# Last instruction of quantising the FFN weights: from VectorE to ScalarE

## The chip, the cores and the metric

The kernel runs on one core of a Trainium2 chip. The metric is the device time of one execution in microseconds. Six names are used for the parts of the core. PE is TensorE (matrix multiplies), and PEld is its loading of weights. DVE is VectorE, ACT is ScalarE, POOL is GpSimd, and SP is SyncE, whose queue (SPq) issues every DMA of this kernel. Each engine carries out its own instructions in order, and waits at an instruction until what that instruction needs has been done by the others.

## The reference

One layer with gated cross-attention and a gated feed-forward part (FFN), for 32 sequences of 224 tokens of width 512, with a context of 750 rows of width 384 for each sequence:

```
x = x + tanh(g_xattn) * attention(layernorm(x), ctx, mask, Wq, Wkv)     # 16 heads of 32
x = x + tanh(g_ffn)   * ffn(layernorm(x), w1, b1, w2, b2)

def weight_quant(w):
    scale = 1.0 / clip(mean(abs(w)), 1e-05)
    return clip(round(w * scale), -1.0, 1.0) / scale
def bitlinear(x, w, b):
    return act_quant(rmsnorm(x)) @ weight_quant(w).T + b
ffn = bitlinear(gelu(bitlinear(x, w1, b1)), w2, b2)
```

The two FFN weights (2048 x 512 and 512 x 2048) are replaced by one of -1, 0, 1 times the mean of their absolute values. The mean is a sum over the whole matrix, so a weight has to be read once for its mean and again to be rounded.

## The kernel before, in words

The work is a loop over 128 steps (32 sequences times 4 groups of 4 heads), written out at build time from line 908 on. Each step takes about 20 us and has six slots, k = 0 to 5. The order of the instructions on every engine is the order of the calls in the code: the wrapper `Ordered` (lines 44 to 52) records every call in program order, which is why nearly all rows of the profile carry the line number 52.

In the even slots, `maxima` (line 308) of the *next* step writes scores to PSUM on PE (tile `sm`), and DVE takes their maximum (tile `mx`, one reduction of about 2.24 us). In the odd slots, `weights` (line 365) of the *current* step writes the scores again on PE (tile `se`), and ACT takes the exponential (tile `p`, 1.66 us), which POOL adds up (tile `acc`, passes of about 2.1 us). `sm` and `se` share one PSUM buffer (pool `ps_s`, line 164). So PE, DVE and ACT pass it round: `sm` waits until ACT has read `se`, and `se` waits until DVE has read `sm`.

In the slots lie further pieces. `k_units` (line 260) computes keys two steps ahead; ACT copies them to `kT`, in slots 0 and 1. `v_piece` (line 276) computes values, which ACT or DVE copies. `q_piece` (line 249) computes queries, multiplied into `qT` by DVE. `turn_max` in slot 0 gives `nT`, copied by ACT, which the `se` of slot 1 needs. `finish` on POOL gives `yo`, and `store` on SP writes it to memory in slot 4. In the first step of a sequence, slot 4 also has `spread` (line 235): SP writes 224 numbers to memory (`r_d`), and reads them back to all partitions (`rb`). These pieces use the four PSUM buffers of pool `ps_m` in turn.

The FFN weights are prepared in the first twelve steps by `weight_units` (line 447). It gives 34 units, and one of them is called in each odd slot, after `weights` of that slot and before its other pieces. First come sixteen units that load a piece of 128 x 1024 numbers (`fetch`, SP) and add up its absolute values (`add_up`, DVE). Then one unit works out the scales. Then sixteen units load each piece again and quantise it (`quantise`, line 486). These last units are numbered 0 to 15 in what follows. They fall on steps 6 to 11: units 0, 3, 6, 9, 12, 15 have slot 1, units 1, 4, 7, 10, 13 slot 3, and units 2, 5, 8, 11, 14 slot 5. (Unit 0 comes in slot 1 of step 6, since the unit ahead of it, with the scales and the first load, has slot 5 of step 5.)

Each unit first issues the load of the piece of the next unit. The pieces lie in the two buffers of tag `h` (line 455). So the load for unit n + 1 waits until unit n - 1 has finished with its piece. `quantise` has three instructions: times the scale and at most 1; at least -1 and plus `MAGIC` (12582912, which rounds to a whole number); and minus `MAGIC`, with the result written in 8 bits to `w1q` or `w2q`. The tile `magic` (line 107) holds -`MAGIC` in each partition. The FFN proper (`Ffn.fill`) starts after these units, and the first matrix multiply that reads `w1q` is at 368 us.

Of the kernel before, what the change touches and what calls it, by code (L numbers as in the profile page):

```python
# [13 lines left out]
AF = mybir.ActivationFunctionType  # L14
ALU = mybir.AluOpType
# [5 lines left out]
MAGIC = 12582912.0  # L21
# [3 lines left out]
def flamingo_gated_layer(  # L25
# [28 lines left out]
    pe, dve, act = Ordered(nc.tensor), Ordered(nc.vector), Ordered(nc.scalar)  # L54
# [52 lines left out]
    magic = const.tile([P, 1], F32, name="magic")  # L107
# [339 lines left out]
    def weight_units():  # L447

        NW = 8
        parts = const.tile([P, 2, NW], F32, name="wparts")  # L450
        tot = const.tile([P, 2], F32, name="wtot")
        held = {}

        def fetch(which, i, tag):
            wl = hp.tile([P, F // 2], F32, tag="h", name=f"{tag}_{which}_{i}")
            if which == 0:
                c, h = divmod(i, NW // NDC)
                n = F * NDC // NW
                sp.dma_start(wl, w1T[c * P : (c + 1) * P, h * n : (h + 1) * n])
                held[tag, which, i] = wl, w1q[:, c, h * n : (h + 1) * n]  # L460
                return
            k = NFC // NW
            sp.dma_start(
                wl.rearrange("p (k d) -> p k d", k=k),
                w2T[i * k * P : (i + 1) * k * P, :].rearrange("(k p) d -> p k d", p=P),
            )
            held[tag, which, i] = wl, w2q[:, i * k : (i + 1) * k, :].rearrange("p k d -> p (k d)")

        def add_up(which, i):
            wl, _ = held.pop(("wa", which, i))  # L470
            dve.tensor_reduce(
                parts[:, which, i : i + 1], wl, AX.X, ALU.add, apply_absolute_value=True
            )

        def mean():
            dve.tensor_reduce(tot, parts, AX.X, ALU.add)
            pm = ps_m.tile([P, 512], F32, tag="m", name="pwm")
            pe.matmul(pm[:, 0:2], ones, tot, start=True, stop=True)
            dve.tensor_scalar(wmean, pm[:, 0:2], 1.0 / (D * F), 1e-5, ALU.mult, ALU.max)
            dve.reciprocal(wscale, wmean)  # L480

            dve.tensor_scalar(w127, wmean, 1.0 / 127.0, None, ALU.mult)
            dve.tensor_tensor(w127[:, 1:2], w127[:, 1:2], tg[:, 1:2], ALU.mult)
            dve.tensor_scalar(b2g, b2g, tg[:, 1:2], None, ALU.mult)

        def quantise(which, i):
            wl, to = held.pop(("wb", which, i))
            dve.tensor_scalar(wl, wl, wscale[:, which : which + 1], 1.0, ALU.mult, ALU.min)
            dve.tensor_scalar(wl, wl, -1.0, MAGIC, ALU.max, ALU.add)
            dve.tensor_scalar(to, wl, -MAGIC, None, ALU.add, saturate=False)  # L490

        every = [(w, i) for w in range(2) for i in range(NW)]
        units = [lambda: fetch(*every[0], "wa")]
        for n, wi in enumerate(every):
            def one(n=n, wi=wi):
                if n + 1 < len(every):
                    fetch(*every[n + 1], "wa")
                add_up(*wi)
            units.append(one)

        def between():
            fetch(*every[0], "wb")
            mean()
        units.append(between)
        for n, wi in enumerate(every):
            def two(n=n, wi=wi):
                if n + 1 < len(every):
                    fetch(*every[n + 1], "wb")
                quantise(*wi)
            units.append(two)  # L510
        return units
# [509 lines left out]
```

## Time and profile before

| | us |
|---|---|
| three runs: median | 3109.46 |
| lowest, highest | 3102.85, 3111.33 |
| the profiled execution: its own time | 3101.86 |
| its span in the trace | 3100.1 |
| PE busy | 2902.6 (94%) |
| POOL busy | 2072.0 (67%) |
| DVE busy | 1745.1 (56%) |
| ACT busy | 1392.6 (45%) |
| stretch 170 to 240: PE, DVE, ACT busy of 70 | 64.16, 51.74, 20.87 |
| stretch 240 to 310: PE, DVE, ACT busy of 70 | 58.87, 46.58, 20.29 |

The profile shows one execution. Its durations and moments are used for sums, and the medians of the runs for what the time is. Times within the trace are counted from the start of the span. The sixteen units of `quantise` lie between 181.7 and 303 us. Outside this stretch no instruction is touched by the change. A row of the timeline gives the start, the duration, the engine, and in square brackets how long the engine had been idle and which instruction ended that. In a row of waits stand the total in us, how often, and the longest.

### The profile page before, as it was taken

To read this page: it belongs to the slowest core of one execution; us is meant where nothing else is said; L and a number is where in the kernel's file an instruction comes from. 1 tells how busy PE (TensorE), PEld (TensorE's weight loads), DVE (VectorE), ACT (ScalarE), POOL (GpSimd) and SP (SyncE) were. 2 spreads that over 40 slices of the span, in tenths; PEclk is the share of its full clock that TensorE was granted. 3 is DMA by queue.
4 is the path that set the end of the run, shared out by engine and by line. 5 is a ranking of instruction groups with operands and counts; after the bars stand their busy time and mean duration, and the time that the engine had idled before them with its cause. 6 is when DMAs were issued, how large, how long until landed. Compare 5 with 4: busy or idle time off the path is not lost.

```text
span 3100.1 us, 62640 instructions
## 1 busy us (share of the span) xinstructions
PE 2902.6 (94%) x26774; PEld 1843.6 (59%) x26774; DVE 1745.1 (56%) x2641; ACT 1392.6 (45%) x1344; POOL 2072.0 (67%) x2675
## 2 busy tenths in 40 slices
PE   8988899999999999999999999899999999999965
PEld 5655556665666666666666666566666656666543
DVE  5566555554655555555555555555555555555545
ACT  2322345454544545454444454545444454544543
POOL 3545767667676776776766767766767777667671
PEclk9999999999999999999999999999999999999987
DMA  4333221232221222221222222122221222222122
GB/s 135 94 102 101 51 43 45 63 71 54 57 59 39 66 62 68 66 50 38 61 54 62 61 71 57 30 69 48 73 61 35 53 68 62 71 64 45 23 51 65
DMA packets 352696, 190.02 MB, mean 61 GB/s; under 512 B 282144, under 2 KB 305056, under 8 KB 352288
## 3 DMA queue, kind: packets, MB, share of 16 engines
q1 hardware_dynamic: 352416, 186.01, 23.7%
q8 instruction: 209, 3.42, 0.5%
q14 instruction: 71, 0.58, 0.1%
HBM read 119.86 MB, written 29.39 MB: 48 GB/s over the span
## 4 chain that ended last, share of the span: by engine, by line
PE 78%; ACT 7%; DVE 5%; POOL 4%; DMA 4%; issue 2%; SPq 1%; ACTq 0%; POOLq 0%; DVEq 0%
PE po L52 16%; PE se L52 13%; PE pk L52 12%; PE sm L52 12%; PE pv_None L52 10%; PE ph L52 6%; ACT p L52 5%; PE pq L52 4%; DVE mx L52 4%; PE pv L52 3%; POOL acc L52 2%; ACT L52 1%; DMA r_d<-ve 1%; POOL xg L52 1%; POOL h L52 1%
## 5 line engine op out<-in xcount | busy, mean ns | idle before, releaser
L52 POOL TENSOR_TENSOR acc<-acc,p 125x896 f32<-125x896 f32 x512 | 1067.1, 2084 | 532.8 <-ACT p L52 512.6
L52 DVE TENSOR_REDUCE mx<-sm 112x4 f32<-112x2000 f32 (+1 forms) x384 | 861.0, 2242 | 627.7 <-PE sm L52 627.0
L52 ACT ACTIVATE p<-se 125x1792 f32<-125x1792 f32 x384 | 639.2, 1664 | 680.8 <-PE se L52 651.4
L52 PE MATMUL pk<-y,wkv_sb 128*128 128x375 f32 x1536 | 543.9, 490 | 9.6 <-DMA y<-in_ctxT 9.6
L52 PE MATMUL sm<-kT,qT 32*112 32x500 f32 (+1 forms) x4096 | 426.9, 508 | 72.2 <-ACT p L52 65.7
L52 POOL TENSOR_TENSOR acc<-p 125x896 f32<-125x896 f32 x128 | 268.9, 2101 | 269.9 <-ACT p L52 269.9
L52 PEld LDWEIGHTS pk<-y,wkv_sb 128*128 128x128 f32 x1536 | 277.3, 191 | 179.3 <-issue 43.0
L52 PE MATMUL pv_None<-wkv_sb,y 128*125 128x256 f32 x1548 | 368.0, 387 | 0.0
L52 PE MATMUL se<-qT,kT 32*125 32x224 f32 x6144 | 361.6, 351 | 0.0
L52 PEld LDWEIGHTS pv_None<-wkv_sb,y 128*125 128x125 f32 x1548 | 280.2, 187 | 131.3 <-issue 92.0
L52 PE MATMUL po<-p,v 125*32 125x224 f32 x6144 | 318.5, 356 | 0.0
L52 PEld LDWEIGHTS se<-qT,kT 32*125 32x125 f32 x6144 | 297.4, 184 | 0.0
L52 PEld LDWEIGHTS sm<-kT,qT 32*112 32x112 f32 x4096 | 159.4, 170 | 231.4 <-ACT p L52 172.7
L52 ACT COPY kT<-pk 128x375 f32<-128x375 f32 x256 | 119.9, 468 | 350.8 <-PE pk L52 350.5
L52 PE MATMUL ph<-w1q,xT 128*128 128x512 fp8e4 x896 | 228.6, 387 | 35.6 <-DMA xT<-xq 35.0
L52 DVE SCALAR_TENSOR_TENSOR h<-ph,qa_am,b_sb 128x512 f32<-128x512 f32 x224 | 165.5, 746 | 165.5 <-PE ph L52 160.4
L52 PEld LDWEIGHTS po<-p,v 125*32 125x32 f32 x6144 | 187.0, 110 | 119.6 <-issue 43.8
L52 PE MATMUL po<-w2q,hT 128*128 128x256 fp8e4 x1792 | 222.4, 280 | 25.5 <-DMA hT<-hq 22.6
L52 PE MATMUL pq<-xTb,wq_sb 128*128 128x224 f32 x1024 | 220.8, 359 | 1.1 <-DVE wq_sb L52 0.6
L52 PEld LDWEIGHTS <-hT 128*128 128x128 bf16 x1792 | 172.3, 100 | 66.4 <-DMA hT<-hq 24.5
L52 PE MATMUL se<-nT,ones 3*125 3x448 bf16 x1536 | 158.1, 401 | 49.2 <-DVE mx L52 42.4
L52 PEld LDWEIGHTS pq<-xTb,wq_sb 128*128 128x128 f32 x1024 | 189.3, 191 | 23.3 <-issue 12.4
(118 smaller groups left out, 2811.4 us busy)
## 6 DMA issues: line engine op xcount, KB each, us to landing
y<-in_ctxT SPq DMA_DIRECT2D x31, 1125.0 KB, 6.8
x<-in_x SPq DMA_DIRECT2D x32, 448.0 KB, 7.6
xTb<-in_xT SPq DMA_DIRECT2D x32, 448.0 KB, 3.8
o_d<-yo SPq DMA_DIRECT2D x512, 28.0 KB, 1.6
xg<-in_x SPq DMA_DIRECT2D x28, 512.0 KB, 3.7
og<-o_d SPq DMA_DIRECT2D x28, 512.0 KB, 4.6
out<-xg SPq DMA_DIRECT2D x56, 256.0 KB, 2.2
wa<-in_w1T SPq DMA_DIRECT2D x8, 512.0 KB, 7.1
```

The costliest lines, as they stand in the source:

```text
L52: return lambda *args, **kw: tc.keep_in_program_order(build(*args, **kw))
```

## The change

The third instruction of `quantise` is issued on ACT, as an activation with the function Identity and `magic` as its bias. It computes what the VectorE instruction computed (the piece plus -`MAGIC`), and writes the same tile in the same 8-bit type. Nothing else is changed.

```
             dve.tensor_scalar(wl, wl, wscale[:, which : which + 1], 1.0, ALU.mult, ALU.min)
             dve.tensor_scalar(wl, wl, -1.0, MAGIC, ALU.max, ALU.add)
-            dve.tensor_scalar(to, wl, -MAGIC, None, ALU.add, saturate=False)
+            act.activation(to, wl, AF.Identity, bias=magic, saturate=False)
```

## The prediction

> **What bounds the kernel now.** I read the busy shares first, then PE's waits, then the timeline of the stretch with the sixteen units. The share, and the wait that matters here:
>
> ```profile
> PE 2902.6 (94%) x26774; PEld 1843.6 (59%) x26774; DVE 1745.1 (56%) x2641; ACT 1392.6 (45%) x1344; POOL 2072.0 (67%) x2675
> ```
>
> ```profile
> PE se L52 <- DVE mx L52: 42.4, 47, 7.8
> ```
>
> PE sets the time; what counts is where PE stands still. Its wait for DVE's `mx` has single cases of up to 7.8 us. Between 170 and 310 us three of them lie right behind `quantise`. The first, from the timeline of 190 to 200 us:
>
> ```profile
> 190.39 0.75 DVE L52 TENSOR_SCALAR wb<-wb,wscale 128x1024 f32<-128x1024 f32 x1 [1.82 <-DMA wb<-in_w1T]
> ...
> 190.58 4.98 POOL L52 TENSOR_TENSOR acc<-acc,p 125x896 f32<-125x896 f32 x2 [4.75 <-ACT p L52]
> 191.18 2.45 DVE L52 TENSOR_SCALAR wb<-wb 128x1024 f32<-128x1024 f32 x1
> ...
> 193.66 2.45 DVE L52 TENSOR_SCALAR w1q<-wb 128x1024 fp8e4<-128x1024 f32 x1
> ...
> 196.03 0.38 DVE L52 TENSOR_TENSOR qT<-pq,rb 128x224 f32<-128x224 f32 x1
> 196.34 2.23 DVE L52 TENSOR_REDUCE mx<-sm 112x4 f32<-112x2000 f32 x1
> ...
> 198.61 0.64 PE L52 MATMUL se<-nT,ones 3*125 3x448 bf16 x4 [4.23 <-DVE mx L52]
> ```
>
> The reader is to see two things. The second and third instruction of `quantise` take 2.45 us each while POOL's two passes run; elsewhere the same instructions take 0.69. And PE waits 4.23 us for a reduction whose input (`sm`, 190.49 plus 1.11) had been there since 191.6. The other two stalls, from DVE's and PE's timelines of the stretch after 236 us:
>
> ```profile
> 244.74 2.52 DVE L52 TENSOR_SCALAR w2q<-wb 128x1024 fp8e4<-128x1024 f32 x1
> 247.18 2.23 DVE L52 TENSOR_REDUCE mx<-sm 112x4 f32<-112x2000 f32 x1
> 259.97 0.75 DVE L52 TENSOR_SCALAR wb<-wb,wscale 128x1024 f32<-128x1024 f32 x1 [10.56 <-DMA wb<-in_w2T]
> 260.75 0.69 DVE L52 TENSOR_SCALAR wb<-wb 128x1024 f32<-128x1024 f32 x1
> 261.48 0.69 DVE L52 TENSOR_SCALAR w2q<-wb 128x1024 fp8e4<-128x1024 f32 x1
> 262.09 2.23 DVE L52 TENSOR_REDUCE mx<-sm 112x8 f32<-112x2000 f32 x1
> ```
>
> ```profile
> 249.46 0.41 PE L52 MATMUL se<-nT,ones 3*125 3x448 bf16 x4 [1.66 <-DVE mx L52]
> ...
> 264.38 0.64 PE L52 MATMUL se<-nT,ones 3*125 3x448 bf16 x4 [7.83 <-DVE mx L52]
> ```
>
> In the second (unit 8) a POOL pass again stretches the third instruction, to 2.52 us. In the third (unit 9) DVE waits for a load; the instruction to be moved is the last thing ahead of `mx`.
>
> **What is removed.** Sixteen DVE instructions: 8 x 0.913 + 8 x 0.922, or 14.7 us busy. Most of it is worth nothing: in thirteen of the units DVE waits for PE again ahead of its next `mx`, or the `se` behind comes no later than usual (0.2 us of waiting). Three places count.
>
> Unit 1. `qT` starts at 193.66 instead of 196.03, so `mx` and `se` come 2.37 us earlier; 1.86 us of the stall are left. After 4.23 us of idle time the granted clock was 0.50 (198 to 202 us), and from `se` to the next `sm` took 203.78 - 198.61 = 5.17 us; the same stretch one step later, at full clock, took 224.16 - 221.11 = 3.05. So 2.12 us more are won if the clock now holds, 4.49 in all. Does it? The Trainium skill ("TensorE: Matmul & The Clock Gate", rules) wants no idle gaps above some 3 us; by it 1.86 is safe. The trace is less kind: after an idle gap of 2.46 us at 34 us the clock was 0.57 (36 to 40 us), while after 1.66 us at 249 it was 1.00 (250 to 254 us). 1.86 is nearer to the latter, so I take 4.49; the lower end is 2.37. The upper end is 6.35 (4.23 + 2.12): the load of unit 1 lands among other transfers, and were it some 0.6 us earlier, DVE's second instruction would start ahead of POOL's pass. The load behind it goes out later now (below), which could do that.
>
> Unit 8. `mx` follows `sm` again (1.17 us from `sm`'s start in the undisturbed steps: 244.54 + 1.17 = 245.71), and `se` could start at about 248.0, 1.45 us earlier. But the next stall waits for a transfer that was issued at 252.93, behind the `r_d` write of 246.03; none of that depends on unit 8's third instruction. PE reaches that stall earlier and waits longer: 0.
>
> Unit 9. `mx` starts when the second instruction ends, at 261.4 instead of 262.09: 0.69. The load itself may come earlier. It stands behind `r_d`, `store` and POOL's `yo`. One small POOL instruction beside unit 7's third instruction took 0.65 us where its like take 0.20, so `yo` is 0.45 earlier without it (between 0 and 0.9, as `yo` itself took 1.02 where it usually takes 0.56, beside unit 8). I take 0.45.
>
> **What is added.** Sixteen ACT instructions of 128 x 1024 with a bias from a tile. The nearest row has the same function, bias tile and size, with 16 bits out:
>
> ```profile
> L52 ACT ACTIVATE xq<-xc,magic 128x1024 bf16<-128x1024 f32 x28 | 32.1, 1147 | 20.7 <-POOL xc L52 19.5 <-DMA o_d<-yo 1.2
> ```
>
> 16 x 1.147 = 18.4 us on an engine that is busy 41 of these 140 us. No trace row has ACT writing 8 bits; I take 1.147 (0.9 to 2.3 as bounds: the mean of the DVE row, and twice the row). The Trainium skill ("ScalarE: Activation LUTs", rules for kernel authors) says to add on VectorE and not on ScalarE. By that rule, with the plain durations, the move loses 16 x (1.147 - 0.694) = 7.2 us if both engines were on the path. Here the row decides otherwise: ACT idles, and POOL's passes stretch the DVE form to 2.45 us. Between the start and 370 us ACT loads a table once, for the tanh at the very start, though Identity (`xc`, 329.90 us) follows the exponential there: no table is loaded for the change.
>
> **The new wait and what is behind it.** The ACT instruction stands after `p` of its slot, and waits for DVE's second instruction. Usually that is done before `p` ends (unit 5: 223.41 against 224.11), so it runs as soon as ACT is free. Behind it:
>
> ```profile
> 222.44 1.67 ACT L52 ACTIVATE p<-se 125x1792 f32<-125x1792 f32 x1 [0.63 <-PE se L52]
> 225.50 0.35 ACT L52 COPY nT<-pn 128x224 bf16<-128x224 bf16 x1 [1.40 <-PE pn L52]
> ```
>
> - Slot 5: `nT`, which the next `se` needs. 224.11 + 1.147 = 225.26, so it is free 0.24 us before `nT` can start. `se` starts at 227.63 and `nT` ends at 225.85, so 1.8 us more are in hand.
> - Slot 1: the copy to `kT` comes 0.85 us later, in unit 9 some 10 us later (262.6 instead of 252.75). The keys are read in the next step, and the PSUM buffer is needed again four pieces later (the value piece from 273.8 us on). Nobody waits.
> - Slot 3: ACT has 4 us free ahead of its next copy. In unit 1 the copy of `v` (194.42) is 0.4 us late, for a buffer that is not next.
>
> Where DVE's second instruction is late, `mx` is behind it on DVE as well and needs 2.24 us, longer than the ACT instruction and `nT` together (1.5).
>
> SP's queue: the load for unit n + 1 now waits for ACT in unit n - 1. That is 0.5 to 0.8 us later (unit 2's load: 184.65 instead of 183.9), at most 2.1 (unit 5's: 211.4 instead of 209.3). Loads land in a median of 4.6 to 5.5 us and are wanted 10 us after that. Behind them in the queue is `store`, which waits for POOL and comes later still. The tightest is unit 13's load, issued at 277.21 behind those of the next sequence: ACT is done with unit 11 at 275.7 + 1.15 = 276.85, 0.36 us before. Cost 0.
>
> **The sum.** 4.49 + 0.69 + 0.45 = 5.63 us. Against the profiled execution: 3101.86 - 5.63 = 3096.2, a ratio of 0.9982. That execution was 7.6 us below the median of the runs, so scaled to the median: 3109.46 x 0.9982 = 3103.8.
>
> **Rivals.** Less than 0.3% (9.3 us) is about what a measurement of this kernel can't tell from no change.
>
> 1. More is won (0.15). The locks between DVE and POOL fall differently in each execution, and the median of the runs is 7.6 us above the profiled one: it may hold more such stalls, in slots 3, where DVE's instructions come just ahead of POOL's passes (unit 13: 289.81 against 289.34). With unit 1's stall gone wholly (6.35) and one more of its kind (4.49): 12 us, 3097.5. Against: the order is fixed, and the trace has one such case among five.
> 2. It is hidden or given back (0.22). The clock drops anyway at 1.86 us, and PE's head start is lost at the next transfer, as I say of unit 8 (the load at 350 us, before a stall of 7.68): between 0 and 2.4 us won, 3107 to 3109.5.
> 3. Slower: ACT writes 8 bits far slower than 16 (0.05). The place is slot 5, where `nT` stands behind it. `nT` must end by 227.55, so an instruction of up to 227.55 - 0.35 - 224.11 = 3.1 us does no harm. Beyond that each of five units delays `se` by the excess. At 4.2 us the gain is eaten; at 6 us it is 5 x 2.9 = 14.5 - 5.6 = 9 us slower, 3118. Against: the row of 1.147, and 2048 elements take ACT 1.997 us with 16 bits out (`hq`) and 1.912 with 32 (`h`), so the width of the output hardly shows.
> 4. Unit 13's load comes late (0.08). Were ACT done with unit 11 2 us later than I say, unit 13's two instructions would both meet POOL's passes, as unit 1's did with 4.1 us of stall and 2.1 of cold clock: 6.2 - 5.6, no gain, 3110.
>
> **How the numbers follow.** The likeliest case, 3103.8, has 0.50. Its own range is 3099 to 3109, from the ends of the unit 1 and unit 9 terms and about 3 us of scatter of a median. A fifth of it, half of rival 1 and little else fall below 3100.1, which is 0.3% faster: 0.1 + 0.09, so 0.20. Above 3118.8 lie most of rival 3 and a tail of rival 4 and of the scatter: 0.07. The rest, 0.73, is within 0.3%. The range for 8 in 10 goes from half of rival 1 to the whole of rivals 2 and 4: 3095 to 3112.
>
> **What would show it.** In the changed profile: 16 ACT rows `w1q<-wb` and `w2q<-wb` of about 1.15 us, none stretched; PE's first stall in this stretch about 1.9 us, with `se` after it at full clock; the stall near 249 about 0.2; the stall of unit 9 about 8 us, since it takes over what unit 8 gives. `nT` and `kT` wait for nothing new. Wrong would be: table loads before 300 us, ACT rows above 3 us, a `se` that waits for `nT`, a longer wait of unit 13 for its load, or a gain in this stretch that is gone by 400 us.

## The result, and the profile after

The changed kernel takes 3102.22 us (median of 22 runs, 3096.14 to 3107.68), the kernel before 3105.9 us (median of 22 runs beside them). The ratio is 0.999, with a 95% interval of 0.9982 to 0.9998. So by the ratio the change gains 3 us (0.6 to 5.6), and the medians lie 3.7 us apart. That is little, but it is a gain. The prediction had said 3103.8 us and a ratio of 0.9982, that is 5.63 us.

The profiled execution after has a span of 3102.6 us, 2.5 *longer* than the one before. Single executions scatter by some 4 us, so the change has to be looked for where it acts. PE's waits in the profile after (total in us, how often, longest):

```profile
PE sm L52 <- ACT p L52: 66.1, 76, 3.1
PE se L52 <- DVE mx L52: 38.9, 48, 7.4
...
PE se L52 <- ACT nT L52: 5.0, 1, 5.0
```

PE's wait for `mx` is 42.4 - 38.9 = 3.5 us shorter, and its wait for `nT` is what it was before (5.0 us, once, in both). The moved instruction costs ACT what the row with 16-bit output said (groups, mean in ns after the busy time):

```profile
L52 ACT ACTIVATE w2q<-wb,magic 128x1024 fp8e4<-128x1024 f32 x8 | 9.1, 1142 | 9.3 <-DVE wb L52 9.3
L52 ACT ACTIVATE w1q<-wb,magic 128x1024 fp8e4<-128x1024 f32 x8 | 9.1, 1141 | 6.4 <-DVE wb L52 6.4
```

Unit 1 in the timeline after, DVE's rows and then PE's:

```profile
192.58 0.75 DVE L52 TENSOR_SCALAR wb<-wb,wscale 128x1024 f32<-128x1024 f32 x1 [1.94 <-DMA wb<-in_w1T]
193.37 2.45 DVE L52 TENSOR_SCALAR wb<-wb 128x1024 f32<-128x1024 f32 x1
195.74 0.38 DVE L52 TENSOR_TENSOR qT<-pq,rb 128x224 f32<-128x224 f32 x1
196.04 2.23 DVE L52 TENSOR_REDUCE mx<-sm 112x4 f32<-112x2000 f32 x1
```

```profile
198.32 0.41 PE L52 MATMUL se<-nT,ones 3*125 3x448 bf16 x4 [1.86 <-DVE mx L52]
198.50 0.98 PE L52 MATMUL se<-qT,kT 32*125 32x224 f32 x16
199.41 3.13 PE L52 MATMUL pq<-xTb,wq_sb 128*128 128x224 f32 x8
```

The second instruction is still stretched to 2.45 us by POOL's pass, the third is gone, and PE waits 1.86 us instead of 4.23. But `pq` then takes 3.13 us, where an undisturbed one takes 1.78: the clock of TensorE fell all the same.

For the comparisons below, the stretch is counted in each trace from DVE's scaling of `b2g` (just ahead of unit 0; 176.00 us in the trace before) to the transposition `oT` of step 11 (306.81), and cut at the `oT` of every step. An undisturbed step takes 20.37 us. Each row is one execution:

| kernel | to step 6 | 6 to 7 | 7 to 8 | 8 to 9 | 9 to 10 | 10 to 11 | sum |
|---|---|---|---|---|---|---|---|
| before | 11.68 | 26.80 | 20.37 | 29.39 | 22.20 | 20.37 | 130.81 |
| before, again | 11.68 | 27.20 | 21.22 | 28.45 | 22.43 | 20.37 | 131.35 |
| after | 11.69 | 23.70 | 21.26 | 27.81 | 22.76 | 20.38 | 127.60 |
| after, again | 11.68 | 23.73 | 20.37 | 27.72 | 23.29 | 20.37 | 127.16 |
| units 1, 8, 9 on ACT | 11.68 | 21.81 | 21.65 | 26.80 | 22.45 | 21.75 | 126.14 |
| the other thirteen on ACT | 11.68 | 27.04 | 20.37 | 27.63 | 23.39 | 20.37 | 130.48 |
| before, no POOL pass at unit 1 | 11.68 | 22.00 | 20.68 | 29.19 | 23.46 | 20.37 | 127.38 |
| after, ACT four times | 11.69 | 24.63 | 21.69 | 27.63 | 23.51 | 21.70 | 130.85 |
| before, early loads | 12.25 | 21.26 | 20.70 | 23.51 | 20.93 | 21.26 | 119.91 |
| after, early loads | 11.45 | 20.38 | 20.37 | 20.38 | 20.38 | 20.37 | 113.33 |
| early loads, one instruction on DVE | 12.24 | 25.48 | 24.03 | 23.71 | 24.43 | 24.36 | 134.25 |

The mean of the two traces before is 131.08, of the two after 127.38: 3.70 us less, about what the runs show.

### The profile page after: what moved, and what is told of

The parts are those of the page before. It is cut to its first block, busy times and chain, and to the rows that moved or that the text cites. A ratio compares the mean times of both kernels' runs of the same rounds, so it can differ in the third digit from the quotient of the medians.

```text
span 3102.6 us, 62652 instructions
## 1 busy us (share of the span) xinstructions
PE 2906.2 (94%) x26774; PEld 1844.6 (59%) x26774; DVE 1732.1 (56%) x2625; ACT 1408.5 (45%) x1360; POOL 2069.4 (67%) x2675
## 3 DMA queue, kind: packets, MB, share of 16 engines
HBM read 119.86 MB, written 29.39 MB: 48 GB/s over the span
## 4 chain that ended last, share of the span: by engine, by line
PE 79%; ACT 6%; DVE 5%; POOL 4%; DMA 3%; issue 2%; SPq 1%; ACTq 0%; POOLq 0%; DVEq 0%
PE po L52 16%; PE se L52 13%; PE pk L52 12%; PE sm L52 12%; PE pv_None L52 10%; PE ph L52 6%; ACT p L52 5%; PE pq L52 4%; DVE mx L52 4%; PE pv L52 3%; POOL acc L52 1%; ACT L52 1%; DMA r_d<-ve 1%; DMA xT<-xq 1%; POOL h L52 1%
## 5 line engine op out<-in xcount | busy, mean ns | idle before, releaser
L52 PE MATMUL se<-nT,ones 3*125 3x448 bf16 x1536 | 158.0, 401 | 45.8 <-DVE mx L52 38.9
```

The lines of the kernel that those rows point to most:

```text
L52: return lambda *args, **kw: tc.keep_in_program_order(build(*args, **kw))
```

## The experiments

The theory (A) is the prediction's: the gain sits where DVE's third instruction stood ahead of a reduction for which PE was waiting, above all in unit 1, where POOL's passes stretched it. The rivals are that any relief of DVE pays (B), and that the loads fall differently in each execution and nothing else was seen (C).

**Both kernels once more.** No edit; a second trace of each.

> The kernel before once more, for a second trace. Theory A: unit 1's second and third instruction are stretched again and step 6 to 7 takes about 26.8 us; the whole stretch is 129 to 132 us. Rival C (scatter of the loads): the stretched instructions lie in other units or none.

> The changed kernel once more, for a second trace. Theory A: step 6 to 7 again takes 23 to 24 us with one stretched DVE instruction in unit 1, or about 20.4 if its load lands ahead of POOL's pass; unit 6's stretched instruction and its stall of 1.16 us, which the first trace of the changed kernel has and the kernel before has not, are chance of a load and mostly absent here. If that stall is there again, it belongs to the change.

Steps 6 to 7 took 27.20 us before and 23.73 after, so the two pairs of traces agree in this step to 0.4 us. Unit 6's stall, new in the first trace after, isn't in the second, and is in the second trace *before* (1.10 us at 238 us): it is chance. Unit 1 differs: its stretched instructions are in all four traces.

**Only the three units, and only the other thirteen.**

```
-            dve.tensor_scalar(to, wl, -MAGIC, None, ALU.add, saturate=False)
+            if which * NW + i in (1, 8, 9):        # and the complement: not in
+                act.activation(to, wl, AF.Identity, bias=magic, saturate=False)
+            else:
+                dve.tensor_scalar(to, wl, -MAGIC, None, ALU.add, saturate=False)
```

> Only units 1, 8 and 9 have their last instruction on ACT; the other thirteen keep it on DVE. The stretch is counted in the trace from DVE's b2g instruction to the oT transposition of step 11: 130.81 us before, 127.60 after. Theory A (the gain sits in the places where DVE's instruction stood ahead of a waiting reduction, unit 1 above all, then unit 9): the oT of step 6 to that of step 7 takes 23.7 us as after the change and not 26.8 as before; the stretch is 127 to 129 us. Rival B (relief of DVE in all sixteen units): three sixteenths of the gain, so 130.2, and 26.2 from step 6 to 7. The whole time can't tell these apart: A 3103, B 3105, within the scatter of some 4 us.

> The complement: units 1, 8 and 9 keep the last instruction on DVE, the other thirteen have it on ACT. Theory A: unit 1's second and third DVE instruction take 2.45 us each beside POOL's passes, PE then waits 4.2 us, and step 6 to 7 takes 26.8 us as before; the stretch is 130 to 131 us. Rival B: thirteen sixteenths of the gain, 128.2 us, and 24.3 from step 6 to 7. Rival C (what was seen is the scatter of the loads from one execution to the next): step 6 to 7 has either length, whatever was moved.

With the three alone, steps 6 to 7 take 21.81 us; with the thirteen alone 27.04, as before. For unit 1 that is A, and against B and C. The whole times are 3099.33 and 3101.76 us, with ratios of 0.9998 (0.999 to 1.0007) and 0.9999 (0.999 to 1.0009), and tell nothing apart, as expected. The first interval allows a gain of at most 3 us, where the stretch of that kernel's one trace is 4.9 us shorter than the mean of the two traces before; so the gain in the stretch isn't confirmed by the whole time. Three things had not been expected. Steps 8 to 9 took 27.63 us with the thirteen, 1.3 less than before (28.92 in the mean), although units 8 and 9 are as before there; under "Unit 9" below stands what this is made of. In the first kernel the instruction that stayed on DVE was stretched in unit 13 (2.48 us), and PE waited 1.32 us behind it: POOL's passes can meet it elsewhere too. And steps 6 to 7 took 1.9 us less than in the changed kernel, although unit 1 is the same there. The clock rows say why (the columns are the stretch in us, its length, the busy time of PE, PEld, DVE, ACT, POOL, then the granted clock, the DMA share and GB/s). The changed kernel, PE idle for 1.86 us until 198.32:

```profile
198.00:200.00 2.00, 1.68 (x22) 1.38 (x22) 1.79 (x8) 0.37 (x1) 0.27 (x1) 0.92 0.19 29
200.00:202.00 2.00, 2.00 (x7) 1.73 (x6) 0.89 (x2) 2.00 (x2) 0.56 (x1) 0.50 0.44 70
202.00:204.00 2.00, 2.00 (x13) 0.68 (x12) 0.46 (x2) 0.33 (x1) 1.92 (x2) 0.73 0.86 266
```

The kernel with the three units, PE idle for 1.38 us until 197.91:

```profile
198.00:200.00 2.00, 2.00 (x25) 1.72 (x25) 1.79 (x8) 0.78 (x1) 0.00 (x0) 1.00 0.28 43
200.00:202.00 2.00, 1.84 (x14) 0.75 (x13) 1.50 (x3) 0.88 (x1) 0.97 (x1) 1.00 0.61 125
202.00:204.00 2.00, 2.00 (x12) 1.10 (x8) 1.89 (x1) 0.34 (x1) 1.92 (x2) 1.00 0.79 229
```

In the first, the clock falls to 0.50 only after the idle time is over. The same stretch of the changed kernel, cut where the clock changes (the first number behind the length is PE's busy time, so PE was idle for 1.86 us of the second row):

```profile
192.85:196.26 3.41, 3.41 (x20) 2.17 (x13) 3.38 (x4) 0.41 (x1) 3.33 (x2) 1.00 0.01 4
196.26:199.67 3.41, 1.55 (x22) 1.20 (x22) 3.21 (x8) 1.25 (x3) 2.01 (x2) 1.00 0.06 9
199.67:203.08 3.41, 3.41 (x12) 2.50 (x15) 1.61 (x3) 2.66 (x2) 1.64 (x1) 0.50 0.62 153
203.08:206.50 3.42, 3.20 (x24) 1.39 (x20) 2.56 (x2) 0.79 (x2) 2.51 (x2) 1.00 0.60 178
```

In all thirteen traces the granted clock is either 1.00 or 0.50, and within a trace every fall lies a whole number of times 3.413 us from every other. Cut into windows by this grid, the traces show when the clock falls: it fell behind 148 windows at full clock, each with at least 1.59 us of PE's idle time in it, and held behind some 11100, none with more than 1.97; between the two figures it went either way. So a gap of about 1.9 us counts if it lies in one window, as here (196.46 to 198.32), and not if the edge of a window cuts it. The kernel with ACT four times (below) has a gap of 1.85 us from 248.65 to 250.50, cut at 249.79 into 1.14 and 0.71, and keeps its clock:

```profile
246.37:249.79 3.42, 2.28 (x12) 1.25 (x9) 2.24 (x1) 3.32 (x4) 3.27 (x2) 1.00 0.04 0
249.79:253.20 3.41, 2.70 (x25) 1.87 (x25) 0.00 (x0) 2.44 (x5) 0.00 (x0) 1.00 0.29 2
```

The gap of 1.38 us in the kernel with the three units is too short wherever it lies. The grid doesn't go with the kernel's work: counted from `b2g`, its edges lie 0.2 to 1.6 us further on, differently in each of the eight traces without early loads.

**No POOL pass beside unit 1.** In the kernel before:

```
-        else:
+        elif (b, g, u) != (1, 2, 1):
             for i in range(2):
                 gp.tensor_tensor(acc, acc, p[:, :, i, :], ALU.add)
```

> The kernel before with the two POOL passes of one slot left out (step 6, slot 3, beside unit 1), so that step's sums of weights are short. Theory A (DVE's instruction is stretched by POOL's pass): unit 1's second and third instruction take 0.69 us each, PE's stall of 4.2 us and the slow clock behind it are gone, step 6 to 7 takes about 20.4 us as an undisturbed step does, and the stretch 124.4. Rival D (something else stretches them, such as the load that lands just then): they still take 2.45 us each, and step 6 to 7 takes 26.8.

DVE's timeline of it:

```profile
193.87 0.75 DVE L52 TENSOR_SCALAR wb<-wb,wscale 128x1024 f32<-128x1024 f32 x1 [2.12 <-DMA wb<-in_w1T]
194.65 0.69 DVE L52 TENSOR_SCALAR wb<-wb 128x1024 f32<-128x1024 f32 x1
195.38 0.69 DVE L52 TENSOR_SCALAR w1q<-wb 128x1024 fp8e4<-128x1024 f32 x1
...
205.72 2.46 DVE L52 TENSOR_SCALAR wb<-wb 128x1024 f32<-128x1024 f32 x1
208.21 2.57 DVE L52 TENSOR_SCALAR w1q<-wb 128x1024 fp8e4<-128x1024 f32 x1
```

Without POOL's passes both instructions of unit 1 take 0.69 us. This is A, and D is out: the load lands just ahead of them here too. PE still waits 1.01 us, for the load itself. Steps 6 to 7 took 22.0 us and not 20.4, by that wait and because POOL's next passes now met unit 3 (205.72 and 208.21; they had not met it in either trace before). The whole time is 0.9985 (0.9974 to 0.9995).

**ACT four times.** In the changed kernel:

```
+            for _ in range(4):
                 act.activation(to, wl, AF.Identity, bias=magic, saturate=False)
```

> The changed kernel with the ACT instruction of each unit issued four times. Four take about 4.3 us in a row (1.14 and three times 1.05). Theory A (an ACT instruction of up to 3.1 us in slot 5 does no harm, beyond that PE's se waits for nT): in the five units of slot 5, se waits about 1.2 us more for nT, 6 us in all, and nothing in slots 1 and 3; and the load of unit 13, which waits for ACT in unit 11, comes some 3 us later, so that both its DVE instructions meet POOL's passes and PE waits another 4 to 6 us. The stretch is 133 to 140 us against 127.6. Rival E (ACT has room for anything here): 127.6. Rival F (ACT was at its limit already): three more instructions of 1.05 us in sixteen units on the path, 50 us more, 178.

The four take 4.69 us in a row. PE's timeline in slot 1 behind units 2, 8, 11 and 14 (the row behind unit 5, at 228.50, also has 1.55 and names another releaser):

```profile
206.81 0.41 PE L52 MATMUL se<-nT,ones 3*125 3x448 bf16 x4 [1.55 <-ACT nT L52]
...
250.50 0.41 PE L52 MATMUL se<-nT,ones 3*125 3x448 bf16 x4 [1.85 <-ACT nT L52]
...
279.64 0.41 PE L52 MATMUL se<-nT,ones 3*125 3x448 bf16 x4 [1.54 <-ACT nT L52]
...
301.34 0.41 PE L52 MATMUL se<-nT,ones 3*125 3x448 bf16 x4 [1.55 <-ACT nT L52]
```

The usual wait there is 0.21 us, so `se` is 1.34 later, and 4.69 - 1.34 = 3.35 us is what an ACT instruction may take in slot 5 without harm; the prediction had worked out 3.1. One of 1.14 is far below. In unit 1, where DVE is late, the four also held up the next exponential (`sm` waited 1.44 us for `p` at 202.00). The other half of the expectation missed: the load of unit 13 was issued 3.04 us behind that of `x` (279.38 and 276.34), where the changed kernel has 0.70 (275.60 and 274.90), so 2.3 us late; but DVE didn't wait for it (unit 13 started at 287.67, right behind other work), nor did POOL's passes stretch its instructions. The stretch took 130.85 us, below the 133 to 140 expected and 3.25 above E's 127.6, and the whole time 1.0006 (0.9995 to 1.0017). The fourfold cost eats the gain and no more.

**Early loads.** In both kernels the load that slot 5 issued is issued in slot 4, ahead of `store`, of the write of `r_d` and of its reading back; `fetch` is taken out of the units and called by the loop:

```
+            if wunits and k in (1, 3, 4):
+                nextload[0]()          # the next load, in the same order as before
             for unit in early:
                 unit()
             if wunits:
                 if k in (1, 3, 5):
                     wunits.pop(0)()    # the unit without its load
```

> The kernel before, with one load in three moved: that of slot 5 is issued in slot 4, ahead of store and of the write and read of r_d, in all 34 units of weight preparation. Theory A (unit 9's stall comes from its load standing behind r_d in SP's queue): DVE's wait of 10.6 us for that load is gone, PE's stall of 7.8 us too and the 2.1 us of slow clock behind it; unit 8's stall of 1.7 us stays, since the DVE instruction stretched by POOL is still there. The stretch from b2g to oT of step 11: 130.8 - 9.9 = 120.9 us. The sums of the first half, with a stall of 6.1 us of the same kind at 165 us, gain 6 to 8 us more: in all 3105.9 - 17 = 3089. Rival G (the load is late because the transfers ahead of it fill the DMA engines): it lands as late as before, nothing is gained.

> The changed kernel with the same loads moved. Theory A (the change's gain at unit 8, 1.45 us, was swallowed by unit 9's late load, and is real once that load is early): the stretch is 120.9 - 3.1 (unit 1) - 1.45 (unit 8) = 116.4 us, that is 4.5 us less than with early loads and the old instruction; in all 3085. Rival H (unit 8's gain is lost in another way): 3.1 us less, 117.8.

With the old instruction: 3082.11 us against 3107.31 before, a ratio of 0.9917 (0.9904 to 0.9931). With the moved one: 3078.99, a ratio of 0.991 (0.9896 to 0.9923). SP's queue in the latter, around what was unit 9's stall:

```profile
218.39 14.14 SPq L52 DMA_DIRECT2D wb<-in_w2T  x3
232.62 1.89 SPq L52 DMA_DIRECT2D o_d<-yo  x4
234.56 0.44 SPq L52 DMA_DIRECT2D r_d<-ve  x1
242.38 0.34 SPq L52 DMA_DIRECT2D rb<-r_d  x1
```

The load now goes out ahead of `store` and `r_d`, and no DVE instruction waits for a load in the whole stretch. G is out. PE's waits in the stretch, first with the old instruction, then with the moved one:

```profile
PE se L52 <- DVE mx L52: 6.0, 10, 1.7
PE sm L52 <- ACT p L52: 2.2, 8, 0.4
```

```profile
PE sm L52 <- ACT p L52: 2.0, 7, 0.4
PE se L52 <- DVE mx L52: 1.2, 6, 0.2
```

Unit 8's stall of 1.7 us, worth nothing while unit 9's load was late, is now on the path and is removed by the change: step 8 to 9 takes 23.51 us with the old instruction and 20.38 with the moved one. That is 3.13 us and not 1.45, since the clock fell to 0.50 for one window (238.27 to 241.68) behind the gap of 1.65 us in the former, which lay within one window. The stretch is 6.6 us shorter by the change, where 4.5 was expected, and of other parts: unit 1's 3.1 are not among them, as its load now lands in time and its instructions miss POOL's passes. The other 3.45 us lie in the slots 1. There the units 0, 3, 12 and 15 now come just ahead of POOL's passes, which stretched their second and third instruction (2.46 and 2.57 us), and PE waited 0.82 us behind each. The early loads by themselves gained 10.9 us in the stretch (9.9 had been expected), which also began 4 to 10 us earlier, at 168 to 172 us.

**The pair again, and a version with one DVE instruction.** For the latter the first two instructions were also replaced:

```
-            dve.tensor_scalar(wl, wl, wscale[:, which : which + 1], 1.0, ALU.mult, ALU.min)
-            dve.tensor_scalar(wl, wl, -1.0, MAGIC, ALU.max, ALU.add)
+            act.activation(wl, wl, AF.Identity, bias=plus, scale=wscale[:, which : which + 1])
+            dve.tensor_scalar(wl, wl, MAGIC - 1.0, MAGIC + 1.0, ALU.max, ALU.min)
```

> The changed kernel with the early loads once more, on one chip with the next kernel and with the one of the early loads before the change, to compare the three. Theory A: the stretch from b2g to oT of step 11 takes 113.3 us again and no wait of PE in it is above 0.4 us; the whole time is 4 to 7 us below the kernel with early loads and the old instruction.

> The kernel before with the early loads once more. Theory A: 119 to 121 us in the stretch, five stretched last instructions, PE's waits for mx of 0.8 to 1.7 us behind them. Rival C (scatter): the difference from the changed kernel with early loads is as small as 1 us or has the other sign.

> The changed kernel with the early loads, and the first two instructions of quantise done in another way: ACT multiplies by the scale and adds 12582912 in one instruction, DVE then clips to 12582911 and 12582913 in one instruction, and ACT takes 12582912 off as in the changed kernel. DVE has one instruction in each unit instead of two, ACT two instead of one. Theory A (with early loads no wait of PE is left in the stretch for a still freer DVE to shorten): 113.3 us or more in the stretch, no gain in time; in slot 5 ACT now has 1.15, a wait of 0.7 and 1.15 ahead of nT, 3.0 in all, just under the limit of 3.1 to 3.3. Rival B (each DVE instruction less is a gain): 16 x 0.7 = 11 us less.

The pair repeats to 0.01 us in the stretch: 113.34 and 119.91. The whole times are 3075.13 and 3082.81 us, 7.7 us apart (3.1 in the first pair, where the trace says 6.6), with ratios to the kernel before of 0.9912 (0.9898 to 0.9926) and 0.9935 (0.9921 to 0.9948). Early loads with the moved instruction beat the kernel before by 0.9%, and so the changed kernel by about 0.8% (not measured side by side).

The version with one DVE instruction missed its expectation by far: 134.25 us in the stretch, and a ratio of 0.9991 (0.9985 to 0.9998), so nearly the whole gain of the early loads is gone. Its waits (total, how often, longest):

```profile
DVE wb L52 <- ACT wb L52: 54.1, 16, 4.4
...
PE se L52 <- DVE mx L52: 20.2, 16, 2.0
```

DVE's instruction now waits for ACT's first one, which stands behind the exponential of its slot; and behind DVE's instruction stands `mx`, for which PE waits. DVE has less to do over the sixteen units (25.5 us busy, where early loads with two instructions have 31.9), and holds PE up in nearly every slot. Its one instruction is longer than the two were where nothing stretched them (1.55 to 1.62 us against some 1.45), but that is at most 3 of the 21 us lost. In the changed kernel it is ACT that waits for DVE, and what stands behind it on ACT isn't wanted yet.

## Why the prediction was right or wrong

- **Unit 1, the stall: right.** From the `sm` at the head of step 6 to the late `se` it took 21.63 us before (198.61 - 176.98) and 19.26 after (198.32 - 179.06), 2.37 less, as worked out. That it is POOL's pass that stretches the instruction is shown by leaving the passes out.
- **Unit 1, the clock: wrong.** This is the step that failed: "1.86 is nearer to the latter, so I take 4.49". The clock fell to 0.50 behind the idle gap of 1.86 us, and again in the second trace (gap 1.88, clock 0.57 and 0.58). From `se` to the next `sm` took 4.16 us and not 3.05, so only 1.01 of the 2.12 us came, and 0.27 of that was lost in the pieces behind. Steps 6 to 7 gained 3.1 us (26.80 to 23.70), not 4.49. What was saved is one of two slow windows: before, the clock was 0.50 for 6.83 us from 196.71, after for 3.41 from 199.67. The prediction asked for the length of the gap alone, where its place in the windows decides as well. A gap of 1.86 us lies within one window of 3.41 in 45% of cases, and 1.59 of it do in 61%; so it was about an even chance (an estimate from these figures). By the rule of some 3 us in the Trainium skill ("TensorE: Matmul & The Clock Gate", section "Why this matters for your kernels") the clock should have held; the measurement decides.
- **Unit 8: right.** Its stall became 0.21 us, the next stall took it all back, and with early loads it counts. The second trace before shows the same without the change: there unit 8's stall is 0.21 us and unit 6 has one of 1.10 instead, and the two steps from 7 to 9 take 49.67 us, where the first trace has 49.76.
- **Unit 9: right in sum, in part by luck.** 0.69 + 0.45 = 1.14 had been summed; steps 8 to 9 took 28.92 us before and 27.77 after, as means of two, 1.15 less. The first term is shown: from DVE's first instruction of unit 9 to `oT` takes 4.27 or 4.28 us in the four traces without early loads that keep the old instruction in unit 9 (the kernel with the thirteen is one) and 3.54 or 3.55 in the four that have ACT's, so 0.73. The second was twice the forecast: from the `oT` of step 8 to the first write of `yo` in SP's queue took 9.34 and 8.30 us before and 7.95 and 7.89 after, 0.9 less. It took 7.94 and 7.88 with the three and with the thirteen as well, of which the former keeps unit 7 on DVE, so the cause given in the prediction isn't shown. And from that write to DVE's start on the load took 15.78 and 15.87 us before and 16.31 and 16.29 after, 0.5 longer, for which no term stood; in all eight traces it lies between 15.3 and 16.3.
- **Not foreseen:** steps 9 to 10, at slow clock behind unit 9's stall, took 22.2 and 22.4 us before and 22.8 and 23.3 after, 0.7 more. It goes with the moment at which the clock came back. From the late `se` to that moment were 4.0 and 4.5 us before, and 5.3 and 6.3 after. The kernel with the three units had 4.5 us and took 22.45; the one with the thirteen had 6.5 and took 23.39; the one without the POOL pass, with the old instruction everywhere, had 6.7 and took 23.46. The step is longer by 0.45 to 0.47 of that time in all seven, whichever instruction the kernel has. So what counts there is where the late `se` falls on the grid, and not the moved instruction by itself.
- **ACT and SP: right.** No table was added, each instruction took 1.14 us, no new wait for `nT` or `kT` appeared, and the later release of the buffers cost nothing. Rival 3 fell with the 1.14. Rival 4's condition, a load of unit 13 some 2 us late, came about with the four instructions (2.3 us), and it cost nothing.
- **The sum.** 5.63 us predicted; 3.70 in two traces each; 3 (0.6 to 5.6) in the runs. The mis-sized term is unit 1 with its clock, 4.49 for 3.1 to 3.5; the slow clock behind unit 9 took back 0.7 more. The predicted time also rested on a median of three runs before that is 3.6 us above that of 22, so that 3103.8 came within 1.6 us of what was measured is luck.

## What to carry to other kernels

Ask of an instruction not how long it takes but what stands behind it on its engine and who waits for that: sixteen instructions were moved, two places gained, and moving the *first* instruction of the same chain to the same idle engine lost 21 us in the stretch, because the busy engine then waited in front of what PE needed. Where one stall follows another that is set by a transfer, price the first at nothing until the transfer is earlier; moving one load in three ahead of a slow write in the queue was worth five to eight times the change, and made the change itself worth nearly twice as much in the stretch. And look for the stretched copies of an instruction (here 2.45 us beside 0.69): they show which other engine it collides with, and that place moves when the timing does. Where the change leaves PE an idle gap of 1.6 to 2 us, take the slow clock behind it as an open chance and not as settled either way.

## What the runs showed of the hardware

- A DVE `tensor_scalar` of 128 x 1024 from SBUF to SBUF in f32 takes 0.69 to 0.75 us in most units, and 2.45 to 2.6 beside a running POOL pass of 2.1 us; with the pass left out it takes 0.69 again.
- TensorE's granted clock is 1.00 or 0.50 in these thirteen traces, and falls on a grid of 3.413 us that differs from one execution to the next. It fell behind windows with at least 1.59 us of PE's idle time, and never held behind one with more than 1.97. So the same gap of 2.46 us at the start of the kernel lowered the clock in six of the thirteen traces and not in the other seven. In those six, one window held at least 1.76 us of idle time.
- ACT writes 8 bits as fast as 16: 1.14 us for 128 x 1024. Four in a row on the same tile take 1.17 each.
- The DVE instruction that clips with two constants (maximum, then minimum) took 1.55 to 1.62 us in all sixteen units, where the forms with a multiplication or an addition take 0.69 to 0.75. Why was not tried.
